# A GRU over 128 steps on one core: the input's block products in two 64-column tiles of the matrix array instead of four 32-column tiles

## The chip, the cores and the metric

One core of one Trainium2 chip runs the whole program. The core has five engines with queues of their own: TensorE (PE in the profile; its weight loads are shown apart as PEld), VectorE (DVE), ScalarE (ACT), GpSimd (POOL) and SyncE (SP), which here only issues DMAs. The metric is the device time of one execution in microseconds (us). Before the change it is 1273.05 us, the median of three runs (1268.3 to 1273.75).

TensorE multiplies a stationary operand, loaded by LDWEIGHTS, with a moving operand, streamed by MATMUL. A profile row such as `MATMUL x<-sums_w,s 128*32 128x192 f32` reads: 128 rows of the array (the contraction), a column tile of 32 columns (the stationary operand's width), a moving operand of 128 partitions by 192 columns, float32.

## The reference

A GRU cell runs over x (64 sequences, 128 steps, 512 features) from the initial state h0 (64 by 512), and its states are added to x:

```
z = sigmoid([x_t, h] @ Wz + bz)
r = sigmoid([x_t, h] @ Wr + br)
c = tanh([x_t, r * h] @ Wh + bh)
h_new = (1 - z) * h + z * c
h_next = tanh(h_new @ Wp + bp) if (t + 1) % 4 == 0 and t < T - 1 else h_new
out[:, t] = x[:, t] + h_new
```

All is float32. The part `x_t @ W` of the three gates does not depend on h, so it can be computed ahead; the part with h is a chain of 128 steps.

## The kernel before

**Layout.** The batch of 64 is split into two lanes of 32 (`V = 32`, `S = 2`). A result with 32 batch rows and 512 features lies in PSUM as 128 partitions: four blocks of 32 partitions (`part(q)`), each with 128 features. To fill the four blocks, one product is written as four matmuls with a stationary operand of 128 by 32, one for each block of 32 columns of the array; `four_tiles` (L273) does this for the products with h, with the same left operand and four slices of a weight.

**The recurrence.** A step (`step`) makes the r and z products with h in seven blocks (`rz`, a Strassen-like scheme that uses sums of weights and of states), the candidate with two full products (`full` with `wc`), and in every fourth step a projection (`full` with `wp`). Between them lie sigmoids, tanhs and element-wise work on ACT and DVE that PE waits for.

**The products with x.** They are made in groups of four steps. Two nested seven-product schemes act on blocks of x (`xT`, the turned x, and its sums on POOL: `s12r`, `o12`, `s56`, `s73`, `s4r`) and blocks of the weights (`wx`, and their sums in `sums_w`). A `Batch` holds two outer products (`ms`); for each it makes seven inner ones (`j` = 1 to 7), and `Batch.unit` (L688) is one of these: contraction 128, for both lanes `h` and for two halves `c` of the moving operand, so four matmuls of 128 by 32 by 192. Lane h and half c go to the partitions `part(2 * h + c)`. The results are taken out of PSUM by ACT and DVE (`Batch.out`), combined on POOL (`add_to`, `with_bias`), and sent by `send` (L782) with four DMAs per block into `gx`, in which the step reads them with partitions ordered as the recurrence needs them.

**The turned x.** `join_x` turns one step's x with a DVE transpose into `xT[g][:, i]`: 128 partitions by 2 by 128 columns, where the 128 columns are two blocks `a` of 64, and each 64 are lane 0's 32 batch rows and then lane 1's 32 (`(a h b)`). `turn_rows` writes the same for the first two steps from a PE transpose. `x_left` takes one lane's 32 columns for the plain products (`plain_gate`, `plain`) of the first four steps.

**The order.** The program is emitted in one fixed order on each engine. `step` emits the recurrence, and at its places calls `fill(n)`, which puts `n` units of the x products into PE's queue there (tables `PLACES` and `HEAD`: in a usual step five or six places of 1 to 3 units), so that PE works while DVE and ACT prepare the next product with h. `flush` puts the copies out of PSUM behind them, and `join_next` puts the transposes of x into DVE's queue between the recurrence's own work. A clock of estimated costs (`UNIT`, `BLOCK`, `FULL`) decides which unit is ready; the change leaves it as it is.

A float32 matmul of the source stands in the profile as two MATMUL records and two LDWEIGHTS records (two passes), so the counts of the profile are twice those of the source.

Of the kernel before, what the change touches and what calls it, by code (L numbers as in the profile page):

```python
# [18 lines left out]
def kernel(  # L19
# [14 lines left out]
    nc = tc.nc  # L34
    B, T, D = x.shape
    H = h0.shape[1]
    P = 128
    S = 2
    V = B // S
# [4 lines left out]
    K = D // P  # L44
# [59 lines left out]
    def part(q):  # L104
        return slice(q * V, (q + 1) * V)
# [94 lines left out]
    for h in range(S):  # L200
        nc.gpsimd.dma_start(
            out=h_rows[:, h, :],
            in_=h0[ts(h, V), :].rearrange("b (q j) -> q b j", q=NQ),
# [28 lines left out]
    def spread(bank_, which):  # L232
        n = len(range(*which.indices(3)))
        v = bank_[:, : n * 2 * J].rearrange("p (i d j) -> p i d j", i=n, d=2)
        for d in range(2):
            for h in range(S):
                for c in range(2):
                    nc.tensor.matmul(
                        v[part(2 * h + c), :, d],
                        lhsT=picks[:, 2 * d + c],  # L240
                        rhs=thirds[:, which],
                        start=d == 0,
                        stop=True,
                        skip_group_check=True,
                    )
        for j, i in enumerate(range(3)[which]):
            nc.scalar.copy(
                bias_x[:, :, :, i, :].rearrange("p n d u -> p d n u"),
                v[:, j].rearrange("p d (n u) -> p d n u", n=C),
            )  # L250
# [84 lines left out]
    xT = {}  # L335

    def new_xT(g):
        if g not in xT:
            xT[g] = two.tile([P, Q4, C, P], F32, tag="xT", name=f"xT_{g}")

    def join_x(g, i):
        new_xT(g)
        src = xr[g] if g < FIRST else xs[g]
        nc.vector.transpose(  # L344
            out=xT[g][:, i].rearrange("p c (a h b) -> p h (c a) b", a=S, h=S),
            in_=src[:, i].rearrange("p h (e k) -> p h k e", k=K),
        )

    def turn_rows(t, bank_):
        new_xT(0)  # L350
        for k in range(K):
            nc.tensor.transpose(
                bank_[:, ts(k, B)],
                x_rows[:, ts(t, D)].rearrange("b (p k) -> b k p", k=K)[:, k],
                ident[:B, :B],
            )
        nc.vector.tensor_copy(xT[0][:, t].rearrange("p c n -> p (c n)"), bank_[:, : K * B])

    def outer(kb, nb, ka):
        return wx[:, kb * S + ka, :, :].rearrange("p g (q n u) -> p n q g u", q=NQ, n=C)[:, nb]  # L360
# [14 lines left out]
    def factor(i, j):  # L375
        return {
            1: lambda: inner(i, 0, 0),
            2: lambda: inner(i, 1, 0),
            3: lambda: inner(i, 1, 1),
            4: lambda: tt[i][:, 2],  # L380
            5: lambda: inner(i, 0, 1),
            6: lambda: tt[i][:, 0],
            7: lambda: tt[i][:, 1],
        }[j]()
# [24 lines left out]
    left = set()  # L409
# [54 lines left out]
    def lhs(g, i, j):  # L464
        if i in (1, 2):
            rows, s = (xT[g][:, 0, i - 1], xT[g][:, 1, i - 1]), lambda n: sx[g, 12][:, n, i - 1]
        elif i in (8, 9):
            rows, s = (xT[g][:, 2, i - 8], xT[g][:, 3, i - 8]), lambda n: sx[g, 34][:, n, i - 8]
        elif i == 4:
            rows, s = (xT[g][:, 2, 1], xT[g][:, 3, 1]), lambda n: sx[g, 4][:, n]  # L470
        else:
            key, tab, n0 = {
                5: ("o12", 56, 0), 6: ("o12", 56, 1), 7: ("o34", 73, 0), 3: ("o34", 73, 1)
            }[i]
            o = sx[g, key][:, n0]
            rows, s = (o[:, 0], o[:, 1]), lambda n: sx[g, tab][:, n, n0]
        if j in (1, 2):
            return rows[0][:, ts(j - 1, B)]
        if j == 4:
            return rows[1][:, ts(1, B)]  # L480
        return s({5: 0, 6: 1, 7: 2, 3: 3}[j])
# [4 lines left out]
    def new_gx(q):  # L486
        if q not in gx:
            gx[q] = one.tile([P, S, C, 2, 3, U], F32, tag=f"gx{q % 2}", name=f"gx_{q}")
            for b in range(2):
                G[2 * q + b] = gx[q][:, :, :, b]  # L490
# [73 lines left out]
    def x_left(t, h, k):  # L564
        g, j = divmod(t, Q4)
        c0, s0 = divmod(k, C)
        return xT[g][:, j][:, c0, s0 * B + h * V : s0 * B + (h + 1) * V]

    def plain_bank(t, h):
        return row[h] if t == 0 else xb[2 * (t % 2 if t > 3 else t == 2) + h]  # L570
# [32 lines left out]
    def plain(t, w=wx):  # L603
        def unit(h, k):
            region = plain_bank(t, h)[:, : 3 * J]
            v = region.rearrange("p (g j) -> p g j", g=3)
            four_tiles(v, x_left(t, h, k), lambda q: w[:, k, :, ts(q, J)], k == 0)
            if k == K - 1:
                bias_products(region, slice(0, 3))

        return [
            (
                lambda h=h, k=k: unit(h, k),
                2,
                (lambda h=h: plain_out(t, h)) if k == K - 1 else None,
            )
            for h in range(S)
            for k in range(K)
        ]

    TERMS = {8: ((8, 1),), 9: ((9, 2),), 10: ((1, 5), (2, 3)), 11: ((8, 5), (9, 3))}
    M = {}

    class Batch:
# [63 lines left out]
        def unit(self, ps, j, m, n):  # L688
            g, i = self.ms[m]
            x_, w_ = TERMS.get(i, ((i, i),))[n]  # L690
            right, left = factor(w_, j), lhs(g, x_, j)
            v = ps[:, m].rearrange("p d (g u) -> p d g u", g=3)
            for h in range(S):
                for c in range(2):
                    nc.tensor.matmul(  # L695
                        v[part(2 * h + c)],
                        lhsT=left[:, ts(h, V)],
                        rhs=right[:, c::2],
                        start=j in (1, 5) and m == 0 and n == 0,
                        stop=True,  # L700
                        skip_group_check=True,
                    )

        def block(self, b, a):
            if self.m is None:
# [56 lines left out]
    def over(g, i, when):  # L762

        uses[g, i] = uses.get((g, i), 0) + 1
        free_at[g, i] = max(free_at.get((g, i), 0), when)
        full_uses = lambda b: 2 if b[1] == 7 or b in ((1, 1), (1, 8)) else 1
        batch = next(b for b in Batch.all if (g, i) in b.ms)
        if all(uses.get(b, 0) == full_uses(b) for b in batch.ms):
            room[batch.n] = max(free_at[b] for b in batch.ms)
# [13 lines left out]
    def send(q, n, g, i):  # L783
        new_gx(q)
        parts = [(h, d) for h in range(S) for d in range(2)]
        for k, (h, d) in enumerate(parts):

            def run(h=h, d=d):
                nc.sync.dma_start(
                    out=gx[q][ts(d, 2 * V), h, n].rearrange("p b g u -> p (b g u)"),  # L790
                    in_=M[g, i][ts(h, 2 * V), d].rearrange("p b g u -> p (b g u)"),
                )

            def then(k=k):
                if k == len(parts) - 1:
                    sent.add((q, n))
                    over(g, i, sync_free + 2700)

            crossing.append((pool_free, run, then))
# [21 lines left out]
    def join_next():  # L821
        for n, (g, i, after) in enumerate(joins):
            if all(a in did for a in after) and (
                g is None or g < FIRST or ("xs", g) in did and lands.get(("xs", g), 0) <= clock
            ):
                del joins[n]
                if callable(i):
                    i()
                    poll()
                    return True  # L830
                join_x(g, i)
                did.add(("join", g, i))
                if i == Q4 - 1 and g >= FIRST:
                    load_xs(g + 2, plain_dmas)
                if i == Q4 - 1 and g == GROUPS - 1:
                    load_raw()
                poll()
                return True
        return False
# [458 lines left out]

    idle(28)
    turn_rows(0, bank["E"])  # L1300
    turn_rows(1, xb[3])
    split_bias()
    idle(4)
    for ks in (range(0, 1), range(1, 2), range(2, K)):
        for t in range(2):
            plain_gate(t, R, ks, bias=ks[-1] == K - 1)
    later_loads()
    join_x(0, 2)
    plain_gate(2, R, range(K), bias=True)
    spread(bank["E"], slice(0, 2))  # L1310
    spread(bank["A"], slice(2, 3))
    h_init = tile_("h", "init", two)
    for h in range(S):
# [15 lines left out]
    for n in (3, 2, 4):  # L1329
        sum_outer(n)  # L1330
    join_x(0, 3)
    sum_rz()
    tick(33000)
# [46 lines left out]
    h, v_1 = h_init, None  # L1380
    for t in range(T):
        if t == 1:
            load_xs(3, plain_dmas)
        h, v_1 = step(t, h, v_1)
# [39 lines left out]
```

## Time and profile before

| | before |
|---|---|
| median of 3 runs | 1273.05 us |
| profiled execution, its time | 1270.18 us |
| its span on the core | 1268.3 us |
| granted TensorE clock, mean | 0.996 |
| PE busy | 1233.8 us (97%) |
| PEld busy | 1131.0 us (89%) |
| DVE busy | 900.8 us (71%) |
| POOL busy | 916.6 us (72%) |
| ACT busy | 565.1 us (45%) |
| DMA, mean rate | 89 GB/s |

The span is the time from the first to the last instruction on the core; the execution's own time has about 2 us more around it. Busy times are unions over the span. A matmul's record is longer than its share of the array: matmuls follow each other before the one ahead has ended, and their ends are modelled. So the starts of the records tell the pace, and the lengths do not. In the timeline, instructions of one kind in a row are merged: a row has the start of the first, the time to the end of the last, and their count.

### The profile page before, as it was taken

The page shows a single profiled execution, that of the slowest core. Times are in us where ns is not written, and L with a number is a line of the kernel's source. Part 1 is how long each engine was busy: PE and PEld are TensorE (multiplying, and loading weights), DVE is VectorE, ACT ScalarE, POOL GpSimd, SP SyncE. Part 2 cuts the span into 40 slices and gives each one's busy share as a digit, 9 for nine tenths or more (in the row PEclk, how much of TensorE's full clock was granted, in tenths as well). Part 3 has the DMA queues.
Part 4 walks back from the last instruction along what each step waited for, and adds up shares of the span by engine and source line. Part 5 has one row for each costly group of instructions (what it writes and reads, how often), then busy time and mean ns, then how long its engine had stood idle before and what let it go on. Part 6 is the DMA issues. An engine that isn't in the chain of part 4 may idle for free.

```text
span 1268.3 us, 85362 instructions
## 1 busy us (share of the span) xinstructions
PE 1233.8 (97%) x37576; PEld 1131.0 (89%) x37576; DVE 900.8 (71%) x2964; ACT 565.1 (45%) x1838; POOL 916.6 (72%) x1045
## 2 busy tenths in 40 slices
PE   7899999999999999999999999999999999999997
PEld 6798999999998999989899999988889999999887
DVE  5656777777776777777777777777777777777665
ACT  1344444444444444444444444444444444444443
POOL 1796787876868778687786868778677786868751
PEclk9999999999999999999999999999999999999999
DMA  7323333333343332333324343332333324333322
GB/s 243 87 51 79 89 92 86 83 92 87 74 102 84 85 90 74 92 96 83 83 71 101 82 102 82 90 89 72 91 82 83 97 73 99 85 90 93 86 61 62
DMA packets 153090, 112.43 MB, mean 89 GB/s; under 512 B 20836, under 2 KB 148976, under 8 KB 152720
## 3 DMA queue, kind: packets, MB, share of 16 engines
q1 hardware_dynamic: 152288, 106.68, 33.2%
q8 instruction: 295, 4.83, 1.7%
q14 instruction: 75, 0.61, 0.2%
q0 software_dynamic: 256, 0.14, 0.0%
q10 hardware_dynamic: 176, 0.16, 0.0%
HBM read 41.36 MB, written 16.78 MB: 46 GB/s over the span
## 4 chain that ended last, share of the span: by engine, by line
PE 95%; issue 2%; DVE 1%; ACT 1%; POOL 1%; DMA 0%; DVEq 0%; POOLq 0%; ACTq 0%
PE x L695 39%; PE bank_B L275 20%; PE bank_C L275 15%; PE bank_A L275 13%; PE bank_E L275 5%; PE x L275 2%; DMA stage<-in_L_cond_bh_dram 0%; POOL wx L308 0%; ACT bank_A L1011 0%; DVE xT L344 0%; DVE h L1234 0%; DVE bank_E L1233 0%; DVE rh L1119 0%; DVE ht L271 0%; POOL stage L191 0%
## 5 line engine op out<-in xcount | busy, mean ns | idle before, releaser
L303 POOL TENSOR_TENSOR mb<-mb,mb 128x768 f32<-128x768 f32 x167 | 304.6, 1832 | 172.5 <-ACT mb L739 82.1
L695 PE MATMUL x<-sums_w,s 128*32 128x192 f32 x2880 | 184.9, 326 | 0.0
L303 POOL TENSOR_TENSOR xr<-xr,h 128x256 f32<-128x256 f32 x127 | 111.3, 876 | 94.8 <-DVE h L1234 94.7
L275 PE MATMUL bank_B<-wrz,ht 128*32 128x128 f32 x4000 | 173.7, 273 | 4.9 <-issue 2.9
L275 PE MATMUL bank_A<-tr,ht 128*32 128x128 f32 x3936 | 168.9, 273 | 1.4 <-issue 0.8
L275 PEld LDWEIGHTS bank_B<-wrz,ht 128*32 128x32 f32 x4000 | 133.0, 110 | 13.4 <-issue 8.8
L275 PE MATMUL bank_B<-wc,rhT 128*32 128x128 f32 x4096 | 142.1, 274 | 2.9 <-DVE rhT L271 0.5
L275 PE MATMUL bank_C<-wc,rhT 128*32 128x128 f32 x4096 | 141.2, 273 | 0.0
L275 PEld LDWEIGHTS bank_A<-tr,ht 128*32 128x32 f32 x3936 | 129.5, 110 | 8.4 <-DVE bank_B L1153 4.2
L275 PEld LDWEIGHTS bank_B<-wc,rhT 128*32 128x32 f32 x4096 | 112.8, 109 | 24.2 <-ACT bank_A L1011 16.0
L695 PE MATMUL x<-sums_w,o 128*32 128x192 f32 x1920 | 124.9, 326 | 1.0 <-issue 1.0
L275 PEld LDWEIGHTS bank_C<-wc,rhT 128*32 128x32 f32 x4096 | 119.8, 110 | 0.5 <-ACT bank_C L1125 0.2
L695 PEld LDWEIGHTS x<-sums_w,s 128*32 128x32 f32 x2880 | 111.3, 110 | 4.9
L1159 DVE TENSOR_TENSOR bank_C<-bank_A,gx 128x256 f32<-128x256 f32 x123 | 53.2, 433 | 82.1 <-PE bank_A L275 82.1
L1011 ACT ACTIVATE bank_A<-bank_B 128x128 f32<-128x128 f32 x123 | 32.2, 262 | 154.6 <-DVE bank_C L1159 151.2
L1119 DVE TENSOR_TENSOR rh<-bank_A,h 128x128 f32<-128x128 f32 x192 | 56.1, 292 | 52.7 <-ACT bank_A L1011 46.2
L725 ACT COPY x<-x 128x384 f32<-128x384 f32 x108 | 50.3, 465 | 86.9 <-PE x L695 86.9
L303 POOL TENSOR_TENSOR mb<-mb 128x768 f32<-128x768 f32 x47 | 86.2, 1834 | 2.5
L731 ACT COPY u<-x 128x384 f32<-128x384 f32 x108 | 51.8, 479 | 78.1 <-PE x L695 78.1
L739 ACT COPY mb<-x 128x384 f32<-128x384 f32 x108 | 52.1, 482 | 77.1 <-PE x L695 73.9
L271 DVE STREAM_TRANSPOSE rhT<-rh 128x128 f32<-128x128 f32 x256 | 79.8, 312 | 9.0
L275 PE MATMUL bank_E<-wrz,ht 128*32 128x128 f32 x1968 | 85.0, 274 | 0.2 <-issue 0.2
(884 smaller groups left out, 3085.6 us busy)
## 6 DMA issues: line engine op xcount, KB each, us to landing
gx<-mb SPq DMA_DIRECT2D x496, 96.0 KB, 2.5
xr<-in_x_dram SPq DMA_DIRECT2D x248, 64.0 KB, 2.8
out_dram<-xr SPq DMA_DIRECT2D x248, 64.0 KB, 2.6
xs<-in_x_dram SPq DMA_DIRECT2D x240, 64.0 KB, 2.9
wx<-in_L_cond_Wz_dram SPq DMA_DIRECT2D x2, 512.0 KB, 6.2
wx<-in_L_cond_Wh_dram SPq DMA_DIRECT2D x2, 512.0 KB, 8.0
wrz<-in_L_cond_Wr_dram SPq DMA_DIRECT2D x2, 512.0 KB, 9.3
wrz<-in_L_cond_Wz_dram SPq DMA_DIRECT2D x2, 512.0 KB, 10.8
```

What stands on the lines that cost most here:

```text
L271: nc.vector.transpose(out=dst, in_=src)
L275: nc.tensor.matmul(region[part(q)], lhsT=left, rhs=rhs(q), start=start, stop=True, skip_group_check=True,)
L303: nc.gpsimd.tensor_add(o, a, b)
L695: nc.tensor.matmul(v[part(2 * h + c)], lhsT=left[:, ts(h, V)], rhs=right[:, c::2], start=j in (1, 5) and m == 0 and n == 0, stop=True, ski ...
L725: nc.scalar.copy(self.a, self.u)
L731: nc.scalar.copy(self.u_sb, self.u)
L739: nc.scalar.copy(self.block(1, 0), runs(self.u))
L1011: nc.scalar.activation(gate_out(dst), gate_in(lane, i), AF.Sigmoid)
L1119: nc.vector.tensor_mul(rh[:, h], r_ps[:, h], h_old[:, h])
L1159: nc.vector.tensor_add(row[1][:, : 2 * J].rearrange("p (n j) -> p n j", n=2), bcast(u_ps), G[t][:, 1, :, :2].rearrange("p n g u -> p n (g ...
```

## The change

Four things are changed together.

1. `Batch.unit`: the loop over the two lanes goes away. The stationary operand has both lanes' 64 columns, and the two halves `c` of the moving operand go to two column tiles of 64 (`ts(c, B)`, partitions 0 to 63 and 64 to 127). One unit has two matmuls of 128 by 64 by 192 where it had four of 128 by 32 by 192.
2. The turned x has its lanes interleaved (`(a b h)` in place of `(a h b)`), written so by the transpose in `join_x` and the copy in `turn_rows`; `x_left` reads each second column.
3. A result's partition is now `64 c + 2 b + h` where it was `32 (2 h + c) + b`. `send` therefore takes each second partition (`h::S`) where it took 64 in a row.
4. `spread`, which lays out the biases for the results, writes `part(2 * c + h)` to match.

The order of the instructions on each engine, the units in each place and the tables are the same as before.

```diff
@@ spread @@
-                        v[part(2 * h + c), :, d],
+                        v[part(2 * c + h), :, d],
@@ join_x @@
-            out=xT[g][:, i].rearrange("p c (a h b) -> p h (c a) b", a=S, h=S),
+            out=xT[g][:, i].rearrange("p c (a b h) -> p h (c a) b", a=S, h=S),
@@ turn_rows @@
-        nc.vector.tensor_copy(xT[0][:, t].rearrange("p c n -> p (c n)"), bank_[:, : K * B])
+        nc.vector.tensor_copy(
+            xT[0][:, t].rearrange("p c (a b h) -> p (c a) h b", a=S, h=S),
+            bank_[:, : K * B].rearrange("p (k h b) -> p k h b", k=K, h=S),
+        )
@@ x_left @@
-        return xT[g][:, j][:, c0, s0 * B + h * V : s0 * B + (h + 1) * V]
+        return xT[g][:, j][:, c0, s0 * B + h : (s0 + 1) * B : S]
@@ Batch.unit @@
-            for h in range(S):
-                for c in range(2):
-                    nc.tensor.matmul(
-                        v[part(2 * h + c)],
-                        lhsT=left[:, ts(h, V)],
-                        rhs=right[:, c::2],
-                        start=j in (1, 5) and m == 0 and n == 0,
-                        stop=True,
-                        skip_group_check=True,
-                    )
+            for c in range(2):
+                nc.tensor.matmul(
+                    v[ts(c, B)],
+                    lhsT=left,
+                    rhs=right[:, c::2],
+                    start=j in (1, 5) and m == 0 and n == 0,
+                    stop=True,
+                    skip_group_check=True,
+                )
@@ send @@
-                    in_=M[g, i][ts(h, 2 * V), d].rearrange("p b g u -> p (b g u)"),
+                    in_=M[g, i][h::S, d].rearrange("p b g u -> p (b g u)"),
```

The next two listings are PE's queue, before and after, at one place in a usual step in the middle of the program. `bank_` rows are products with h (the r and z blocks, then the candidate with `wc`), `x_` rows are units of the x products; `32x128 x8` is eight matmuls with a stationary width of 32 and 128 moving columns.

```order
L275 MATMUL bank_B<-wrz,ht 32x128 x8
L275 MATMUL bank_E<-wrz,ht 32x128 x8
L275 MATMUL bank_A<-tr_86,ht 32x128 x8
L695 MATMUL x_100<-wx,xT_7534 32x192 x8
L695 MATMUL x_102<-sums_w,s_9_7197 32x192 x4
L275 MATMUL bank_A<-tr_87,ht 32x128 x8
L275 MATMUL bank_B<-wrz,ht 32x128 x8
L695 MATMUL x_102<-sums_w,s4r_7436 32x192 x4
L275 MATMUL bank_C<-tr_88,ht 32x128 x8
L695 MATMUL x_99<-sums_w,s_9_7197 32x192 x4
L695 MATMUL x_99<-sums_w,s4r_7436 32x192 x4
L275 MATMUL bank_B<-wc,rhT_7937 32x128 x16
```

After the change the same place reads:

```order
L275 MATMUL bank_B<-wrz,ht 32x128 x8
L275 MATMUL bank_E<-wrz,ht 32x128 x8
L275 MATMUL bank_A<-tr_86,ht 32x128 x8
L697 MATMUL x_100<-wx,xT_6710 64x192 x4
L697 MATMUL x_102<-sums_w,s_9_6409 64x192 x2
L275 MATMUL bank_A<-tr_87,ht 32x128 x8
L275 MATMUL bank_B<-wrz,ht 32x128 x8
L697 MATMUL x_102<-sums_w,s4r_6622 64x192 x2
L275 MATMUL bank_C<-tr_88,ht 32x128 x8
L697 MATMUL x_99<-sums_w,s_9_6409 64x192 x2
L697 MATMUL x_99<-sums_w,s4r_6622 64x192 x2
L275 MATMUL bank_B<-wc,rhT_7069 32x128 x16
```

Nothing has moved; each x row has half the matmuls at twice the width, and the queue now goes from width 32 to width 64 and back six times in these twelve rows. Counted over PE's whole queue, there are 637 stretches of x products with something else on both sides, so 1274 changes of width.

On DVE, the place where `join_x` stands inside the recurrence, at the end of a step with a projection; `ht` rows are the turned state that PE's next product needs. Before:

```order
L1234 TENSOR_TENSOR h_7449<-bank_E,keep_7300 128x128
L271 STREAM_TRANSPOSE rhT_31p<-h_7449 128x128
L344 STREAM_TRANSPOSE xT_7534<-xs_6119 128x2x4x32
L271 STREAM_TRANSPOSE ht<-h_31p 128x128
L344 STREAM_TRANSPOSE xT_7534<-xs_6119 128x2x4x32
```

After the change:

```order
L1236 TENSOR_TENSOR h_6633<-bank_E,keep_6506 128x128
L271 STREAM_TRANSPOSE rhT_31p<-h_6633 128x128
L344 STREAM_TRANSPOSE xT_6710<-xs_5459 128x2x128
L271 STREAM_TRANSPOSE ht<-h_31p 128x128
L344 STREAM_TRANSPOSE xT_6710<-xs_5459 128x2x128
```

The transposes stand where they stood; the form of their output is another, with a step of two elements along the lanes.

## The prediction

> **What bounds the kernel now.** I read the page's busy times first, then the chain that ended last, then the windows and the timeline of a usual step.
>
> ```profile
> span 1268.3 us, 85362 instructions
> PE 1233.8 (97%) x37576; PEld 1131.0 (89%) x37576; DVE 900.8 (71%) x2964; ACT 565.1 (45%) x1838; POOL 916.6 (72%) x1045
> PE 95%; issue 2%; DVE 1%; ACT 1%; POOL 1%; DMA 0%; DVEq 0%; POOLq 0%; ACTq 0%
> ```
>
> PE is the bound: 95% of the chain is PE, and the other engines have a quarter of the span or more to spare. A busy PE need not be a PE at its peak, so the pace matters. A stretch in the middle, PE alone (start, time to the end of the last, merged):
>
> ```profile
> 610.46 0.65 PE L275 MATMUL bank_A<-tr,ht 128*32 128x128 f32 x16
> 610.89 0.86 PE L695 MATMUL x<-wx,xT 128*32 128x192 f32 x16
> 611.54 0.54 PE L695 MATMUL x<-sums_w,s 128*32 128x192 f32 x8
> 611.87 0.65 PE L275 MATMUL bank_A<-tr,ht 128*32 128x128 f32 x16
> 612.31 0.65 PE L275 MATMUL bank_B<-wrz,ht 128*32 128x128 f32 x16
> ```
>
> From start to start, 16 records of 128 columns take 0.43 us (610.46 to 610.89) and 16 of 192 columns take 0.65 us. Four records, one in each block of 32 columns, thus take 0.109 and 0.163 us. The ratio is that of 192 to 128, so the four blocks stream side by side and the moving columns alone set the pace. The kernel's products of x, all of them in one row of a window over the span:
>
> ```profile
> 0.00:1268.30 1268.30, 656.93 (x12208) 453.28 (x12208) 1.00 0.35 89
> ```
>
> 12208 records are 3052 groups of four; at 0.163 us they are 497 us. Between the products of x and those with h there is no gap: 611.54 to 611.87 is 0.33 us for two groups, the same pace, with the width staying 32.
>
> **The change, part by part.**
>
> *Half the matmuls at twice the width.* A group of four records of 32 columns becomes two of 64. The moving columns stay 192 a pass and two tiles fill the array as four did, so if the tiles still run side by side a group still takes 0.163 us: 0 us.
>
> *Weight loads of 64 columns.* The loads hide behind the matmuls only while one takes less than 0.163 us. The records:
>
> ```profile
> L695 PEld LDWEIGHTS x<-sums_w,s 128*32 128x32 f32 x2880 | 111.3, 110 | 4.9
> L352 PEld LDWEIGHTS x<-ident,x_rows x4: 213/213/213, 4.8 to 5.2; 64*128 64x128 f32 x4
> ```
>
> ```profile
> 14.58 0.30 PE L238 MATMUL bank_A<-thirds,picks 96*32 96x128 bf16 x8
> 14.64 0.19 PEld L275 LDWEIGHTS bank_B<-wx,xT 128*32 128x32 f32 x8
> 14.69 0.30 PE L275 MATMUL bank_B<-wx,xT 128*32 128x128 f32 x4
> ```
>
> A load's record is 110 ns for 32 columns, but the array is held for less: here a float32 load begins at 14.64 and its matmul at 14.69, 0.05 us later. Twice 0.05 is 0.1 us, under 0.163, and a line through 110 ns at 32 and 213 ns at 128 columns gives 144 ns at 64, under it too. So I take 0; the other end is twice the record, 220 ns, or 57 ns more for each of 3052 groups: 174 us. I stay near the first, since a start seen 0.05 us after the load tells more than a record that overlaps its neighbours. The Trainium skill's page TensorE: Matmul & The Clock Gate, section LDWEIGHTS, puts a load at its columns divided by 1.2 GHz, which as an estimate is 53 ns for 64 columns; by that figure too the sum has 0 here.
>
> *Changes of width.* Before, nearly every matmul works in 32-column tiles; after, PE's queue changes between 32 and 64 at 1274 places. The trace of before has one change of shape without a semaphore wait in it, at the start, where transposes in a tile of 64 rows by 128 columns are followed by dummy matmuls in 32-column tiles:
>
> ```profile
> 4.93 0.63 PE L352 MATMUL x<-ident,x_rows 64*128 64x64 f32 x4
> ```
>
> ```profile
> 5.28 0.28 PE L352 MATMUL x<-ident,x_rows 64*128 64x64 f32 x1
> 5.49 0.10 PEld L255 LDWEIGHTS <-zeros 128*32 128x32 bf16 x4
> 5.49 0.40 PE L255 MATMUL bank_B<-zeros 128*32 128x512 bf16 x4
> ```
>
> (The second answer is a window that holds only the last of the four transposes.) The transposes start 0.117 us apart ((5.28 - 4.93) / 3), and the next matmul starts 0.21 us after the last of them: 0.09 us more than the pace. Its weights are not loaded ahead either, as those at 14.64 were: load and matmul both stand at 5.49, when the transpose should have been through. That looks like an array that empties before the shape changes. After such a stop a float32 load is exposed as well, and the trace has that from a start after a wait:
>
> ```profile
> 6.48 0.14 PEld L275 LDWEIGHTS bank_B<-wx,xT 128*32 128x32 f32 x3 [0.89 <-DVE xT L357]
> 6.51 0.27 PE L275 MATMUL bank_B<-wx,xT 128*32 128x128 f32 x1 [0.62 <-DMA wx<-in_L_cond_Wr_dram]
> ```
>
> 0.03 us for 32 columns, so up to 0.06 us for 64, on average 0.045 us. One change then costs from 0.09 us (115 us in all) to 0.135 us (172 us); I take 0.11 us, as part of the load seems already within the 0.09: 1274 x 0.11 = 140 us. The low end is 0: the shape there changes in its rows as well, and a transpose precedes it, so it may not be the same case. The Trainium skill's page TensorEngine Tiling (Array Packing), section Tiling Modes, says that changing the tiling mode, and not just the tile, drains TensorE. It gives no price; by it the sum is the 140 us worked out from the rows above, and without it, taking the row as the transposes' own, the sum would have 0 here. The row agrees with the page as far as one row can.
>
> Nothing covers such a stop: in the middle of the span PE is busy nearly all the time.
>
> ```profile
> 600.00:700.00 100.00, 98.88 (x3065) 91.90 (x3059) 72.59 (x242) 46.05 (x150) 74.06 (x84) 1.00 0.35 86
> ```
>
> PE's idle time there is 1.1%, so at most some 10 us of the stops could fall into waits that PE has anyway. No engine that PE waits for becomes later; they gain time.
>
> *Fewer instructions.* 6104 matmuls and 6104 loads fewer, of 75152: 16%. PE idles on "issue" in these rows of the waits (us in total, times, the longest):
>
> ```profile
> PE x L275 <- issue: 4.9, 2, 2.6
> PE x L695 <- issue: 4.5, 11, 1.0
> PE bank_B L275 <- issue: 2.9, 6, 1.1
> ```
>
> The first is two waits of the start, which the change leaves. Of the other 7.4 us 16% are 1 us; the bounds are 0 and all 7.4 us. I take 1 us, a gain.
>
> *The transposes and copies with a step of two.*
>
> ```profile
> L344 DVE STREAM_TRANSPOSE xT<-xs 128x256 f32<-128x256 f32 x120 | 78.2, 656 | 0.0
> L271 DVE STREAM_TRANSPOSE rhT<-rh 128x128 f32<-128x128 f32 x256 | 79.8, 312 | 9.0
> ```
>
> `join_x` already reads with a step of four, at 2.56 ns an element, against 2.44 ns where both sides lie in a row. A step on the other side should cost no more: 126 transposes by 31 ns are 4 us of DVE, hidden by its idle 28%. Were they twice as slow, 83 us on DVE, part would stand ahead of the turned state that PE waits for; I take 0. `turn_rows` has two copies, and `x_left` loads each second column for products of the first four steps only; the transposes at 4.93 already load with a step of four: 0.
>
> *The crossing with each second partition.* 496 DMAs of 96 KB, 2.5 us to landing, with runs of the same 1536 bytes. PE never waits for them directly: 0 (were a landing doubled, POOL and `gx` would be 2.5 us later, where a step takes 1268 / 128 = 10 us).
>
> *Sum*, from the profiled execution's 1270.18 us, which lies 2.9 us under the median: 1270.18 + 0 + 0 + 140 - 1 = 1409 us. The engines' slack takes little of it; I say 1405.
>
> **The rivals.**
>
> *The array doesn't empty between widths* (the other side). Then only the 1 to 7 us of issue time are left: 1263 to 1270 us, against 1270.18. For it: the pace doesn't change where a product with h follows one with x at another moving width (611.87). Against it: 5.28 to 5.49. It decides where a change costs less than 0.005 us (6.4 us over 1274). 0.5%, or 6.4 us, is about what a measurement of this kernel can tell from no change. Chance 0.21: 0.07 for faster than that bound, 0.14 for within it.
>
> *The loads of 64 columns take twice the record.* 220 ns a group instead of 163: 1270 + 174 = 1444 us. For it: the record is 110 ns, and 32-column loads start every 109 ns. Against it: 14.64 to 14.69. Chance 0.06.
>
> *The array empties to the end of the record, and the load comes after it whole.*
>
> ```profile
> L695 PE MATMUL x<-sums_w,s 128*32 128x192 f32 x2880 | 184.9, 326 | 0.0
> L275 PE MATMUL bank_B<-wrz,ht 128*32 128x128 f32 x4000 | 173.7, 273 | 4.9 <-issue 2.9
> ```
>
> A record is 163 ns longer than the pace (326 - 163, 273 - 109), and with the load's 110 ns a change costs 0.27 us: 1270 + 348 = 1618 us. Against it: the dummy's load at 5.49 stands before the transpose's record ends (5.28 + 0.28). Chance 0.07.
>
> *The two tiles of 64 don't run side by side.* 3052 x 0.163 = 497 us more, 1767 us. Nothing in the trace speaks for it, four tiles do. Chance 0.03.
>
> **How the numbers follow.** The forecast has 0.63: 1405 us, its own range 1380 to 1450. The range that should hold 8 in 10 takes in the case without stops at the low end and the loads' case at the high one: 1260 to 1480 us leaves out 0.10 for the two dear cases and a few hundredths of each side. Slower by over 0.5%: 0.63 + 0.06 + 0.07 + 0.03 = 0.79; within: 0.14; faster: 0.07.
>
> **What would show it.** In the timeline of after, the first x matmul behind a product with h, and the first product with h behind an x row, should start about 0.1 us later than the pace of 0.109 or 0.163 us would have it, with the weight load late too; PEld's busy share falls, and the waits of PE for ACT and DVE shrink. Within a stretch of x rows two records should start each 0.163 us; 0.22 would show the loads as the bound. If starts go on without a step at the changes of width, the forecast is wrong by its one large term, and the time is that of before. L344 at 656 ns and the crossing at 2.5 us show the rest right.

## The result and the profile after

The changed kernel takes 1410.74 us (median of four runs, 1409.84 to 1413.12), the kernel before 1273.4 us beside it: a ratio of 1.1077, 95% interval 1.1023 to 1.1132. It is 137 us slower (130 to 144 us by the interval); the forecast was 1405.

The page of after, its span, busy times and chain:

```profile
span 1409.8 us, 73154 instructions
PE 1387.4 (98%) x31472; PEld 1038.6 (74%) x31472; DVE 902.6 (64%) x2964; ACT 568.5 (40%) x1838; POOL 912.1 (65%) x1045
PE 97%; DVE 1%; issue 1%; POOL 1%; DMA 0%; ACT 0%; DVEq 0%; POOLq 0%; ACTq 0%
```

PE is the bound as before, busy for 154 us more though it has 16% fewer instructions; DVE, ACT and POOL work as long as they did. In a window in the middle (PE, PEld, DVE, ACT, POOL busy, then the clock and the DMA share and rate):

```profile
600.00:700.00 100.00, 100.00 (x2268) 74.49 (x2262) 65.69 (x218) 40.81 (x134) 68.76 (x81) 1.00 0.26 79
```

PE reads 100% busy and yet issues a quarter fewer records than before, where the halved x matmuls alone would make 16%; the clock is 1.00. So the 137 us do not stand anywhere as idle time of PE. They stand between the starts. PE and its weight loads over the same stretch of after, each in its own answer of the timeline:

```profile
610.35 0.64 PE L275 MATMUL bank_A<-wrz,ht 128*32 128x128 f32 x16
610.92 0.87 PE L697 MATMUL x<-sums_w,xT 128*64 128x192 f32 x8
611.62 0.49 PE L697 MATMUL x<-sums_w,s 128*64 128x192 f32 x4
612.05 0.32 PE L275 MATMUL bank_B<-wrz,ht 128*32 128x128 f32 x4
```

```profile
610.35 0.38 PEld L275 LDWEIGHTS bank_A<-wrz,ht 128*32 128x32 f32 x16 [0.28 <-DVE xT L344]
610.92 0.52 PEld L697 LDWEIGHTS x<-sums_w,xT 128*64 128x64 f32 x8 [0.20 <-issue]
611.46 0.31 PEld L697 LDWEIGHTS x<-sums_w,s 128*64 128x64 f32 x4
612.05 0.16 PEld L275 LDWEIGHTS bank_B<-wrz,ht 128*32 128x32 f32 x8 [0.28 <-DVE ht L970]
```

Sixteen records with h took 0.43 us before and 0.57 here (610.35 to 610.92). The twelve x records are six pairs; at 0.163 us they would take 0.98 us, and they take 1.13 (610.92 to 612.05). At each change of width the loads start with the first matmul, where before they ran a pass ahead. The releasers in brackets are not the cause: a DVE transpose of x cannot hold up a load from `ht`; the profile names the last semaphore that it saw, and "issue" where there was none.

From the starts of all groups of side-by-side matmuls between 75 and 1235 us, taken from the trace of after (start of one group to start of the next, median, count):

```
a pass with h (128 columns) to the next       109 ns  x4034
a pass with x (192 columns) to the next       163 ns  x1536
x to h, across the change of width            262 ns  x561    163 + 99
h to h, first pass behind the change          133 ns  x561    109 + 24
h to x, across the change of width            222 ns  x560    109 + 113
x to x, first pass behind the change          213 ns  x560    163 + 50
```

The tenth and the ninetieth percentile lie within 1 ns of each of these medians. A change from x to h costs 99 + 24 = 123 ns, one from h to x 113 + 50 = 163 ns, on average 143 to 144 ns (the medians are whole ns), and 1274 of them cost 183 us. That is 46 us more than the kernel lost. The rest of the account is in the kernel before: over the same window its starts lie 47 us behind the two paces in sum; in after, what is left beside the changes of width is 3 to 4 us. Of the 47 us some 28 stand in 63 gaps of over 164 ns, the longest of 1.3 us, and the rest in several hundred smaller ones. The page sees only a part of it as idle time of PE. Its busy time in this window, in the kernel before and then in after:

```profile
75.00:1235.00 1160.00, 1144.50 (x34976) 1.00 0.35 86
```

```profile
75.00:1235.00 1160.00, 1158.14 (x25952) 1.00 0.26 76
```

That is 15.5 us of idle time before and 1.9 us after; the other 32 us of the kernel before lie under records that overlap.

The other rows of after that the prediction named (the x load, the x matmul, the transposes of x, and the crossing):

```profile
L697 PE MATMUL x<-sums_w,s 128*64 128x192 f32 x1440 | 171.7, 335 | 0.0
L697 PEld LDWEIGHTS x<-sums_w,s 128*64 128x64 f32 x1440 | 92.7, 136 | 32.8 <-issue 21.0
L344 DVE STREAM_TRANSPOSE xT<-xs 128x256 f32<-128x256 f32 x120 | 76.3, 640 | 0.0
gx<-mb SPq DMA_DIRECT2D x496, 96.0 KB, 2.5
```

A load of 64 columns has a record of 136 ns and fits behind a pass of 163; the transposes with a step of two take 640 ns where they took 656; a crossing lands in 2.5 us as it did.

### The profile page after: what moved, and what is told of

The parts are those of the page before. It is cut to its first block, busy times and chain, and to the rows that moved or that the text cites. A ratio compares the mean times of both kernels' runs of the same rounds, so it can differ in the third digit from the quotient of the medians.

```text
span 1409.8 us, 73154 instructions
## 1 busy us (share of the span) xinstructions
PE 1387.4 (98%) x31472; PEld 1038.6 (74%) x31472; DVE 902.6 (64%) x2964; ACT 568.5 (40%) x1838; POOL 912.1 (65%) x1045
## 4 chain that ended last, share of the span: by engine, by line
PE 97%; DVE 1%; issue 1%; POOL 1%; DMA 0%; ACT 0%; DVEq 0%; POOLq 0%; ACTq 0%
PE x L697 42%; PE bank_B L275 20%; PE bank_C L275 15%; PE bank_A L275 14%; PE bank_E L275 4%; PE x L275 2%; DMA stage<-in_L_cond_bh_dram 0%; POOL wx L308 0%; DVE h L1236 0%; DVE bank_E L1235 0%; DVE ht L271 0%; POOL stage L191 0%; POOL xr L303 0%; DVE bank_B L1144 0%; DVE bank_C L271 0%
## 5 line engine op out<-in xcount | busy, mean ns | idle before, releaser
L697 PE MATMUL x<-sums_w,s 128*64 128x192 f32 x1440 | 171.7, 335 | 0.0
L275 PE MATMUL bank_B<-wrz,ht 128*32 128x128 f32 x4000 | 158.4, 276 | 4.2 <-issue 2.6
L275 PE MATMUL bank_A<-tr,ht 128*32 128x128 f32 x3936 | 155.5, 276 | 0.5 <-DVE bank_B L1155 0.5
L275 PEld LDWEIGHTS bank_B<-wrz,ht 128*32 128x32 f32 x4000 | 105.0, 109 | 38.6 <-ACT u L733 12.2
L275 PEld LDWEIGHTS bank_B<-wc,rhT 128*32 128x32 f32 x4096 | 105.2, 109 | 35.2 <-ACT bank_E L1013 28.6
L275 PEld LDWEIGHTS bank_A<-tr,ht 128*32 128x32 f32 x3936 | 102.5, 109 | 34.7 <-issue 21.7
L697 PE MATMUL x<-sums_w,o 128*64 128x192 f32 x960 | 117.3, 339 | 0.0
L697 PEld LDWEIGHTS x<-sums_w,s 128*64 128x64 f32 x1440 | 92.7, 136 | 32.8 <-issue 21.0
L275 PEld LDWEIGHTS bank_C<-wc,rhT 128*32 128x32 f32 x4096 | 115.1, 110 | 1.1 <-issue 0.9
L1153 DVE TENSOR_TENSOR gx<-bank_E,gx 128x256 f32<-128x256 f32 x123 | 52.2, 424 | 56.9 <-PE bank_E L275 54.1
```

The source lines that it names most:

```text
L275: nc.tensor.matmul(region[part(q)], lhsT=left, rhs=rhs(q), start=start, stop=True, skip_group_check=True,)
L697: nc.tensor.matmul(v[ts(c, B)], lhsT=left, rhs=right[:, c::2], start=j in (1, 5) and m == 0 and n == 0, stop=True, skip_group_check=True,)
L1153: nc.vector.tensor_add(n1, bcast(e_ps), n1)
```

## The experiments

**The layout without the wide tiles.** `e1_layout32` keeps the interleaved x, `x_left`, `spread` and the strided crossing of the changed kernel, and goes back to four 32-column tiles:

```diff
             for c in range(2):
-                nc.tensor.matmul(
-                    v[ts(c, B)],
-                    lhsT=left,
+                for b in range(2):
+                    nc.tensor.matmul(
+                        v[part(2 * c + b)],
+                        lhsT=left[:, ts(b, V)],
                         ...
```

> The changed kernel with its interleaved layout, its strided crossing and its x_left, but each unit again as four matmuls in 32-column tiles (both halves of the 64 columns, one after the other). Theory (the changes of width cost it all): no change of width is left, 1268 to 1280 us, the same as before. Rival (the layout takes part of the 137 us: transposes and crossings with a step of two): above 1280 us by its part, up to 1410.

Measured: 1266.83 us, against 1268.11 us for the kernel before on the same chip; ratio 0.9991 (0.9966 to 1.0017). The interleaving, the transposes with a step and the crossing by each second row cost nothing that can be measured. The whole loss is with the 64-column tiles.

**64-column tiles everywhere.** `e2_all64` puts the products with h into 64-column tiles too, so that behind the first steps no width is left to change to. It uses two of the four slices of each weight, so it computes something else than the reference; the order and the pace of PE's work stay:

```diff
-            four_tiles(region, lT[:, ts(k, V)], lambda q: w[:, k, ts(q, J)])
+            two_tiles(region, lT[:, ts(k // 2, 2 * V)], lambda q: w[:, k, ts(q, J)])
```

(The same is done in `rz` and `gate_product`; `two_tiles` issues two matmuls of 64 columns with `rhs(0)` and `rhs(2)`.)

> The changed kernel, with the products with h in two 64-column tiles as well: the stationary operand is 64 columns of the same turned state, and of the four slices of the weight only two are used, so what it computes of the recurrence is not the reference's; the amount of PE time, the order and the waits are kept. Theory (the changes of width cost it): after the first steps no change is left, 1230 to 1275 us. Rival (64-column tiles are slow in themselves, by their loads of 136 ns): products with h, which have a pace of 109 ns, would now be bound by the load, some 6300 groups by 27 ns or more, so 1410 + 170 us or more where the tile is the cost, and 1273 + 170 = 1443 us where both are.

Measured: 1237.08 us; ratio to the kernel before 0.9752 (0.9716 to 0.9787). The x products are exactly those of the changed kernel, and 174 us of its time are gone (the two ran on different chips, on which the kernel before took 1273.4 and 1268.11 us). So it is not the 64-column tile that costs, nor its load, but the change between it and the 32-column tile. The starts say the same: x to h is 163 ns here, h to x 109 ns. The loads of 64 columns, of which a pair ran behind each pass of 109 ns, are no bound either, although their record is longer than the pass:

```profile
L287 PE MATMUL bank_B<-wc,rhT 128*64 128x128 f32 x2048 | 137.1, 274 | 2.5 <-DVE rhT L271 0.5
L287 PEld LDWEIGHTS bank_B<-wc,rhT 128*64 128x64 f32 x2048 | 114.3, 136 | 19.0 <-ACT bank_A L1024 6.8
```

That it falls 31 us below the kernel before is the other half: the gaps between the starts sum to 19 us in the same window, not 47.

**The price of a change by itself.** `e4_probe` puts dummy matmuls of zeros at the start of the kernel before, in groups of three products of one shape and three of another, four times a pair:

```diff
         ...
+        for a, b in (("32", "64"), ("64", "128"), ("32", "128"), ("64", "64r"), ("b32", "b64")):
+            for _ in range(4):
+                some(a)
+                some(b)
```

> The kernel before with dummy matmuls of zeros at its start that alternate between two shapes, three products each, four times: 32 and 64 columns, 64 and 128 columns, 32 and 128 columns (float32), 64 columns on 128 and on 64 rows (float32), 32 and 64 columns in bfloat16. Theory (any change of the tile's columns empties the array): starts 0.10 us over the pace at each change, and the second pass late by the load. If the stop belonged to 32 beside 64 alone, 64 to 128 would go on at pace. If only columns count, a change of rows would go on at pace.

Measured, from the starts in its trace (192 moving columns; a float32 pass is 163 ns, a bfloat16 pass 82 ns):

```
change                            last start of the old shape      first pass of the new shape
                                  to first start of the new        longer than its pace by
32 -> 64 columns, float32                 256 ns                         50 ns
64 -> 32 columns, float32                 256 ns                         24 ns
64 -> 128 columns, float32                256 ns                        102 ns
128 -> 64 columns, float32                256 ns                         51 ns
32 -> 128 columns, float32                256 ns                        102 ns
64 columns, 128 -> 64 rows                256 ns                         50 ns
64 columns, 64 -> 128 rows                252 ns                         51 ns
32 -> 64 columns, bfloat16                176 ns                         25 ns
64 -> 32 columns, bfloat16                176 ns                         10 ns
```

Each of these changes of shape, in columns or between 128 and 64 rows, up or down, stops the array for 93 ns over the pace of the last pass (256 - 163; 176 - 82 is the same to 1 ns; only 64 to 128 rows has less, 252 - 163 = 89). Not every change in rows does: in the kernel before, matmuls of 96 rows are followed by matmuls of 128 rows at the same width (14.58 to 14.69, shown with the prediction), and there the starts go on at the pace, 55 and then 56 ns apart. Behind the stop the first load of the new shape is exposed: in float32 24, 50 and 102 ns for 32, 64 and 128 columns, 0.8 ns a column; in bfloat16 10 and 25 ns for 32 and 64, half of that or less. The starts of side-by-side tiles are about 7 ns apart after a stop, so it counts from the last of two or of four. That gives the kernel's two prices: 93 + 7 + 24 = 124 ns from x to h, where the old shape has two tiles, and 93 + 20 + 50 = 163 ns from h to x, where it has four.

**Stops without a change of width.** The first form, `e3_stops`, was to put 175 us of dummy matmuls at the same 1274 places of the kernel before, into a free part of `bank_A`:

```diff
         ...
+        for _ in range(3 if to == "x" else 2):
+            for q in range(NQ):
+                nc.tensor.matmul(
+                    bank["A"][part(q), 3 * J :],
+                    lhsT=picks[:, q],
+                    rhs=thirds[:, 0],
                     ...
```

> The kernel before, with dummy bfloat16 matmuls of the bias operands in 32-column tiles into a free part of PSUM at each change between x and h: three groups of 55 ns ahead of each x stretch, two ahead of each h stretch, so 637 x 0.275 = 175 us of PE time without a change of width. Theory (about 45 us of small stops in the kernel before are hidden behind any longer stop): 1270 + 175 - 45 = 1400 us, near the changed kernel. Rival (nothing hides, the price of a change is 0.11 us as predicted): 1270 + 175 = 1445 us.

Measured: 1795.74 us, and it tells nothing on the question. The waits of PE show why (us in total, times, the longest):

```profile
PE bank_A L281 <- DVE rh L1138: 182.4, 244, 1.1
PE bank_A L281 <- DVE bank_B L1172: 62.2, 122, 0.9
PE bank_A L281 <- DVE bank_B L1161: 49.8, 120, 0.4
```

The dummies wait for readers of other columns of the same bank, so x products could no longer cover the recurrence: 294 us of waits of its own making.

`e7_stops` puts the dummies behind the first product of each stretch, into the region just written, and adds zeros:

```diff
         ...
+        for _ in range(times):
+            nc.tensor.matmul(
+                o, lhsT=nil, rhs=rhs, start=False, stop=True, skip_group_check=True
+            )
```

> The kernel before with dummy bfloat16 matmuls that add zeros, one of 384 columns (160 ns) behind the first unit of each x stretch and two of 128 (110 ns) behind the first product of each h stretch, all in one 32-column tile and into the region that was just written, so with no wait of their own: 637 x 0.27 = 172 us of stops without a change of width. Theory (stops hide the 47 us that PE loses in small gaps before: they give waits and the supply of instructions time to catch up): 1268 + 172 - 40 = 1400 us. Rival (nothing hides): 1440 us.

Measured: 1409.56 us; ratio to the kernel before 1.115 (1.1114 to 1.1185), which of 1268 us is 146 us for 172 us of stops. So 26 us are hidden, less than the theory's 40 and more than the rival's 0, with an interval of about 5 us. The dummies stand in the first tile of 32 columns, and the starts show that the other three tiles run on by a pass before they wait, so these stops are not as complete as those of a change of width. The starts say more than the time: between 75 and 1235 us they lie 163 us behind the two paces, and the stops of the 562 stretches in there are 152 us of it, if they take their full 0.27 us a stretch, which is an estimate. Some 11 us of other gaps are then left, where the kernel before has 47.

**Fewer changes.** `e5_after_merged` takes the one-unit place out of each step of the changed kernel, and `e6_before_merged` does it in the kernel before:

```diff
-        0: (1, 3, 3, 1, 2, 0, 0),
-        1: (3, 3, 3, 1, 2, 0, 0),
+        0: (0, 4, 3, 0, 3, 0, 0),
+        1: (3, 3, 3, 0, 3, 0, 0),
         ...
```

> The changed kernel with the fourth place for x products in a step (1 unit between the gates of the two lanes) given to the fifth, and in the steps after a projection the first given to the second as well: the same units in fewer stretches, 1006 changes of width in place of 1274. Theory (0.144 us a change, as the trace of after has it): 268 x 0.144 = 39 us less, so 1372 us, and more by whatever PE then waits for, which the same merge in the kernel before shows. Rival (the cost goes with the 64-column products and not with the changes): about 1410 us, or more by the waits.

> The kernel before with the same merge of places, which in 32-column tiles changes no width. Both theories: 1268 us plus the waits that the missing unit no longer covers, between 0 and 0.4 us in each of 123 steps, so 1268 to 1320 us. The difference between this one and the merged changed kernel is then that of 1006 changes: by the theory 1006 x 0.144 = 145 us less what the stops hide.

Measured: 1413.52 us (ratio 1.1182, 1.1141 to 1.1222) and 1284.99 us (ratio 1.0173, 1.0135 to 1.0211). By time alone the first looks like the rival: 268 changes fewer and no gain. The trace divides it. The unit that was taken away had covered the wait of the product `bank_C` for DVE's sum; PEld's waits for it in the kernel before and in the merged kernel before, and then in the changed kernel (where they are the stops ahead of this product) and in the merged changed kernel:

```profile
PEld bank_C L275 <- DVE bank_C L1159: 10.7, 65, 0.4
PEld bank_C L275 <- DVE bank_C L1159: 42.2, 118, 0.4
```

```profile
PEld bank_C L275 <- DVE bank_C L1161: 29.3, 105, 0.4
PEld bank_C L275 <- DVE bank_C L1161: 44.5, 119, 0.4
```

From the starts, that product comes 302 ns late in both merged kernels, in 105 of the 123 steps (in 15 of the others a unit still stands right ahead of it), and its first load of 24 ns is exposed behind the wait: 34 us. With the waits behind the projections, where the first place went too, and some smaller ones, the merged changed kernel has 41 us of waits more, against 268 x 0.144 = 39 us saved. (The merged kernel before loses only 22 us, since others of its gaps shrink.) Each change left still costs 262 - 163 + 24 or 222 - 109 + 50 ns. A place with one unit thus pays 0.29 us for two changes and covers 0.33 us of a wait; it makes next to no difference whether it is there.

**The number of instructions.** Two runs cut each x matmul into two of 96 columns, `e8_after_halves` in the changed kernel and `e9_all64_halves` in the one with 64 columns throughout:

```diff
+            for d in range(2):
                 for c in range(2):
                     nc.tensor.matmul(
-                        v[ts(c, B)],
+                        v[ts(c, B), d],
                         lhsT=left,
-                        rhs=right[:, c::2],
+                        rhs=right[:, 2 * d + c],
                         ...
```

> The changed kernel with each matmul of an x unit cut into two of 96 moving columns: still 64-column tiles and 1274 changes of width, but as many matmuls and loads as before the change. Pace by the trace: two passes of 82 ns for one of 163, so some 3052 x 2.5 = 8 us more by the fixed part. Theory A (the stops themselves give the supply of instructions time to catch up): 1410 + 8 = 1418 us. Theory B (part of the 47 us was saved by the smaller number of instructions, not by the stops): 1418 plus up to 20 us, 1425 to 1440 us.

> The kernel with 64-column tiles throughout (its recurrence is not the reference's, as there), with the x units' matmuls cut into two of 96 columns: 25280 matmul records in place of 19176, and no changes of width. If PE's small gaps without stops come from the number of instructions, it is 1237 + 8 plus 5 to 15 us, 1250 to 1260 us; if they come from the four tiles of 32 columns, 1237 + 8 = 1245 us.

Measured: 1419.46 us (ratio 1.1184, 1.1129 to 1.1239) and 1245.47 us (ratio 0.9816, 0.9773 to 0.9859): 8.7 and 8.4 us more than without the cut. The pairs ran on different chips, so these differences hold to some us only; the starts give 82.5 ns for a pass of 96 columns and 162.5 for one of 192 (means), so two for one are 2.5 ns more, 7.6 us for 3052. So the halved number of x matmuls saves nothing that shows, with the stops or without them. The gaps of the kernel before go away where the stops are (3 to 4 us left in after), and mostly where 32-column tiles are not (19 us left with 64 columns throughout). Whether these need the four narrow tiles, or the full number of matmuls with h, these runs don't tell apart.

## Why the prediction was right

*PE as the bound, the pace set by the moving columns, two tiles side by side like four.* Right: x passes start every 163 ns in after.

*Weight loads of 64 columns: 0.* Right. The line through the two records gave 144 ns; the record is 136. What decided was that the array is held for less than the record: 50 ns where a load is exposed, and in `e2_all64` such loads keep up with a pass of 109 ns. The page TensorE: Matmul & The Clock Gate of the Trainium skill, section LDWEIGHTS, has columns divided by 1.2 GHz, 27, 53 and 107 ns as estimates for 32, 64 and 128 columns. The probe's 24, 50 and 102 ns in float32 agree to 5 ns, while its 10 and 25 ns in bfloat16, for 32 and 64 columns, are half of the page's or less.

*Changes of width: 1274 x 0.11 = 140 us.* The mechanism was right: a stop at each change of width, and the rival of an array that doesn't empty is gone. The row it was read from was good to some ns: 0.21 - 0.117 = 0.093 us there (210 - 120 = 90 ns by the single starts), 93 ns in the probe. The Trainium skill's page TensorEngine Tiling (Array Packing), section Tiling Modes, says that a change of the tiling mode drains TensorE. The starts agree: each change comes 93 ns late. But the size of the term failed: it is 0.144 us a change and 183 us in all, above the upper end of 0.135 us that the prediction gave. The step that failed is "part of the load seems already within the 0.09". No load is within it: the first load comes on top in full, 24 or 50 ns, and so does the spread of the tiles' starts, 7 or 20 ns, which was not counted at all.

*"Nothing covers such a stop", at most some 10 us.* Wrong, and this is why the sum came out: 183 us of stops cost 137 us. PE's idle time of 1.1% was taken for all that it loses. A record is longer than the pace, so PE reads busy across a gap of up to 164 ns, and only what a longer gap has beyond that stands as idle. The starts showed 47 us of gaps in 1159 us of the kernel before, of which 15.5 us were idle time on the page. `e7_stops` shows that stops of another kind hide 26 of 172 us; that the stops of a change of width hide nearly all of the 47 is what the account of after leaves (3 to 4 us of other gaps), but no run took the hiding apart further. Two errors of about 45 us, of opposite sign, left 1405 beside 1410.74: that the time came so close is luck, that it rose by well over 100 us through the changes of width is not.

*Fewer instructions: 1 us.* `e8_after_halves` puts it at nothing that shows: 8.7 us for doubling the x matmuls again, of which the passes' own pace makes 7.6. *The layout and the crossing: 0.* Right (`e1_layout32`).

*What would show it:* starts about 0.1 us late at each change, loads late with them, PEld's share down (89% to 74%): all seen. The waits of PE for ACT and DVE were to shrink; of the waits that the page sees there was little to shrink, and PEld's waits grew, being the stops under other names; the longest in total (us, times, the longest) has 0.2 us each:

```profile
PEld x L697 <- issue: 111.8, 562, 0.6
```

## What to carry to other kernels

A change in the shape of the array's tile, in columns or between 128 and 64 rows, costs a fixed stop and then one exposed load (here 93 ns, and in float32 0.8 ns a column), so a wider tile for one part of the work must be worth more than the changes to and from the other part; with stretches of 1 to 3 units of 0.33 us, 0.29 us a stretch is never earned back when the pace stays the same. Keep one width throughout, or count the changes in the queue before choosing two. And read the starts of matmuls, not their busy time: the stops, and most of the gaps they covered, were invisible in a PE that was 97 to 100% busy.

## What the runs showed that had not been expected

The stop is 93 ns to 1 ns for all changes of columns tried, in float32 and bfloat16, and about as long (89 to 93 ns) between 128 and 64 rows, while 96 rows beside 128 go on without one. The program with 64-column tiles throughout is 2.5% faster than the kernel before (1237.08 us) at the same pace of each pass; a kernel of that kind that computes the reference would have to make the products with h for both lanes at once, which the recurrence's order by lanes doesn't allow as it stands, and it wasn't tried. A dummy matmul into unused columns of a PSUM bank waited for the bank's other readers and cost 294 us of waits (`e3_stops`).
